# A depthwise convolution divided differently among TensorE, VectorE and ScalarE with GpSimd, in two state-space layers

## The chip, the cores and the metric

The kernel runs on one core of a Trainium2 chip, in fp32 but for a few bf16 operands. The metric is the device time of one execution in microseconds (us). The kernel before took 1493.69 us, the median of three runs (1493.68 to 1497.0). A profile is one further execution; its times are used for the stages.

## The reference, cut to what matters

Two layers are applied in turn to an image of 64 x 64 pixels with 96 channels. Each normalizes its input, projects it to 192 channels `x_val` and 192 gates `z`, convolves `x_val` with its own 3 x 3 filter in each channel, takes `silu`, runs four selective scans over the pixels, normalizes, multiplies by `silu(z)`, projects back and adds the input. The change concerns the projection, the convolution and the gates:

```python
xz = x @ in_proj_w
x_val, z = (xz[..., :D_INNER], xz[..., D_INNER:])
xc = jnp.transpose(x_val, (0, 3, 1, 2))
xc = jax.lax.conv_general_dilated(xc, conv_w, (1, 1), 'SAME', dimension_numbers=('NCHW', 'OIHW', 'NCHW'), feature_group_count=D_INNER) + conv_b[None, :, None, None]
x_val = jax.nn.silu(jnp.transpose(xc, (0, 2, 3, 1)))
...
y = y * jax.nn.silu(z)
return y @ out_proj_w
```

## The kernel before, in words

**Stages.** The program is one serial course: loading, `head` of layer 0, `near_scans` (the scans of layer 0, in a short form), `tail`, `head` of layer 1, `scans` (the long main part) and `last_tail`. Both heads are the same code, called with `l` = 0 and 1. In the profile a head begins with the first `in` matmul, at 23.84 us for layer 0 and at 204.83 us for layer 1.

**Tiles of a head.** The 192 channels times 4096 pixels are three blocks `b` of 128 partitions (64 channels, upper and lower half of the image), each in four chunks `c` of 512 pixels (eight rows). So there are twelve chunks (b, c). For each:

- `project(b, c)` multiplies the input by the weights `ws` on TensorE into a PSUM bank from `room` (tile `in`). `room` has two banks, tags `p0` and `p1`, one buffer each.
- `padded(b, c)` copies that bank into `pad[b]`, which has a border of one pixel on each side. ScalarE does it but for two chunks, which VectorE does.
- `borders(b)`, once for a block, brings the border rows from the neighbouring half or chunk with four DMAs on SP's queue, issued once the block's last `padded` is done.
- The nine taps of the convolution are done in one of three ways. `tap_pe` (TensorE): nine matmuls of shifted views of `pad` with diagonal weights `diag`, summed in a bank (tile `cp`). `tap_dve` (VectorE): nine multiply-adds into a PSUM accumulator `acc` (two buffers). `tap_act` and `tap_pool`: ScalarE multiplies a shifted view into a tile `tap` (three buffers), GpSimd adds it to the chunk's sum. The taps are ordered with the centre row first; taps 3 to 8 read border rows.
- `silu` (ScalarE) takes the sum to `u[b]`.
- `gate(b, c)` is a second projection on TensorE into a bank (tile `z`); `gated(b, c)` takes its `silu` on ScalarE (tile `sz`, eight buffers) and writes it to `szd` in DRAM over SP's queue.

**Shares before.** TensorE convolves chunks 0, 1, 2 of block 2, VectorE chunks (0, 0) to (0, 3) and (1, 0), (1, 1), in pairs, ScalarE with GpSimd (2, 3), (1, 3) and (1, 2). Projections take the banks by `c % 2`; all `cp` tiles are in `p0`, all gates in `p1`. Gates stand between the taps of TensorE, in the ratio of four to nine.

**What sets the order.** Every step of `head` is entered with `at(t, step, ...)`, t being a planned time in about microseconds. At the end the steps are sorted by t and issued; `Ordered` (line 271, which is why the profile puts these instructions on L271) keeps each engine's queue in that order. [...]

**What follows a head.** It returns six `start_y` products on GpSimd (`y = u * ds`, 128 x 1024 each). In layer 0 `near_scans` issues them after its own GpSimd memsets; in layer 1 `scans` issues them first of all. After that come the first matmuls on `u`: `nu` in layer 0, `pj` in layer 1. At the start of `scans`, `su` is made on VectorE (tile `wl` ahead of it) and spread to `du` by DMAs on GpSimd's queue; `sp` is spread to `dt` on SP's queue; GpSimd makes a part of the operands `bT` of the scans. The scans proper are tile `h` on VectorE.

Of the kernel before, what the change touches and what calls it, by code (L numbers as in the profile page):

```python
# [25 lines left out]
HT = TC // 2  # L26
NCH = L // TC
SR = HT // HW
# [16 lines left out]
def two_ss2d_layers(  # L45
# [60 lines left out]
    for h in range(2):  # L106
        t = const.tile([128, 128], F32, name=f"wide{h}")
# [117 lines left out]
    def layer_weights(l, queue):  # L225

        w = {"st": st[l], "next": st[1]}
        w["ipw"] = wts.tile([DM, 2 * DI], F32, name=f"ipw{l}")
        queue.dma_start(out=w["ipw"], in_=ipw[l])
        v = w["v"] = wts.tile([128, 3, NV], F32, name=f"v{l}")  # L230
        op = w["op"] = wts.tile([128, 3, DM], F32, name=f"op{l}")
        for half in HALF:
            queue.dma_start(out=v[half], in_=vec[l].rearrange("(b p) n -> p b n", b=3))
        for half in HALF:
            queue.dma_start(out=op[half], in_=opw[l].rearrange("(b p) n -> p b n", b=3))
        w["ds"] = wts.tile([128, 3], F32, name=f"ds{l}")
        nc.vector.reduce_sum(w["ds"], v[:, :, V_D : V_D + 4], axis=AX.X)
        return w
# [26 lines left out]
    class Ordered:  # L265
# [7 lines left out]
    pe, act, dve, pool, sp = (  # L273
        Ordered(e) for e in (nc.tensor, nc.scalar, nc.vector, nc.gpsimd, nc.sync)
    )
# [991 lines left out]
    def head(l, xT, w):  # L1267

        ipw_s, v, ds = w["ipw"], w["v"], w["ds"]
        with ExitStack() as sc:  # L1270
# [4 lines left out]
            pad = [cv.tile([128, NCH, SR + 2, HW + 2], F32, name=f"pad{l}_{b}") for b in range(3)]  # L1275
# [13 lines left out]
            W2 = HW + 2  # L1289

            def room(name, tag):
                return cvp.tile([128, HT], F32, tag=f"p{tag}", name=name)
# [21 lines left out]
            live = {}  # L1314

            def project(b, c):
                ps = live["in", b, c] = room(f"in{l}_{b}_{c}", c % 2)
                for h, half in enumerate(HALF):
                    g = 2 * c + h
                    pe.matmul(  # L1320
                        ps[half], ws[:, 64 * b : 64 * b + 64], xT[:, g * 512 : (g + 1) * 512],
                        start=True, stop=True,
                    )

            def padded(b, c):
                copy = dve.tensor_copy if (b, c) in ((0, 2), (0, 1)) else act.copy
                copy(
                    pad[b][:, c, 1 : SR + 1, 1 : HW + 1],
                    live.pop(("in", b, c)).rearrange("p (r w) -> p r w", w=HW),
                )  # L1330
# [9 lines left out]
                sp.dma_start(out=t[h1, :n, SR + 1, row], in_=t[h0, 1:, 1, row])  # L1340

            def gate(b, c):
                ps = live["z", b, c] = room(f"z{l}_{b}_{c}", 1)
                for h, half in enumerate(HALF):
                    g = 2 * c + h
                    pe.matmul(
                        ps[half], ws[:, DI + 64 * b : DI + 64 * b + 64],
                        xT[:, g * 512 : (g + 1) * 512], start=True, stop=True,
                    )
# [8 lines left out]
            def weight(b, i, j):  # L1358
                k = V_CW + 3 * i + j
                return v[:, b, k : k + 1]  # L1360

            def source(b, s, i, j):
                return pad[b][:, s, i : i + SR, j : j + HW]
# [9 lines left out]

            def tap_pe(b, c, k):
                if k == 0:
                    live["cp", c] = room(f"cp{l}_{b}_{c}", 0)
                i, j = taps[k]
                pe.matmul(
                    live["cp", c].rearrange("p (r w) -> p r w", w=HW), diag[:, 3 * i + j, :],
                    source(b, c, i, j), start=(k == 0), stop=(k == 8),  # L1380
                )

            def tap_dve(b, c, k):
                i, j = taps[k]
                o = i * W2 + j
                if k == 0:
                    live["acc", b, c] = cvp.tile(
                        [128, 3 * HT], F32, tag="acc", name=f"acc{l}_{b}_{c}", bufs=2
                    )[:, 0 : 2 * SR * W2]
                acc = live["acc", b, c]  # L1390
                acc = acc.rearrange("p (c t) -> p c t", c=2)[:, :, 0 : SR * W2 - 2]
                of = pad[b].rearrange("p c r w -> p c (r w)")[:, c : c + 2, o : o + SR * W2 - 2]
                wk = weight(b, i, j)
                if k == 0:
                    dve.tensor_scalar_mul(acc, of, wk)
                else:
                    dve.scalar_tensor_tensor(acc, of, wk, acc, ALU.mult, ALU.add)
# [15 lines left out]
            def at(t, step, *args):  # L1413
                steps.append((t, len(steps), partial(step, *args)))

            t = 0.0
            for b, order in ((0, (2, 3, 1, 0)), (2, (3, 2, 1, 0)), (1, (3, 2, 1, 0))):
                for c in order:
                    at(t, project, b, c)
                    at(t + 1.0, padded, b, c)  # L1420
                    t += 1.0
                at(t + 0.05, borders, b)

            for n in range(39):
                c, k = divmod(n * 9 // 13, 9)
                if n * 9 % 13 < 9:
                    at(t, tap_pe, 2, c, k)
                    if k == 8:
                        at(t + 1.0, silu, 2, slice(HT * c, HT * (c + 1)), partial(whole, ("cp", c)))
                else:  # L1430
                    z = n - (n * 9 // 13 + 1)
                    at(t, gate, z // NCH, z % NCH)
                    at(t + 0.95, gated, z // NCH, z % NCH)
                t += 0.87

            t = 2.6
            for b, c, k0, k1 in (
                (0, 2, 0, 3), (0, 0, 0, 3), (0, 2, 3, 9), (0, 0, 3, 9), (1, 0, 0, 9)
            ):
                for k in range(k0, k1):  # L1440
                    at(t, tap_dve, b, c, k)
                    t += 1.35
                if k1 == 9:
                    at(
                        t + 0.1, silu, b, slice(HT * c, HT * (c + 2)),
                        lambda b=b, c=c: live.pop(("acc", b, c)).rearrange(
                            "p (c r w) -> p c r w", r=SR, w=W2
                        )[:, :, :, 0:HW],
                    )

            t = 6.6
            for b, c, k0, k1 in (
                (2, 3, 0, 3), (1, 3, 0, 3), (2, 3, 3, 9), (1, 3, 3, 9), (1, 2, 0, 9)
            ):
                for k in range(k0, k1):
                    if k == 0 and (b, c) == (1, 3):
                        t = 10.6
                    at(t - 1.5, tap_act, b, c, k)
                    if k:
                        at(t, tap_pool, b, c, k)  # L1460
                        t += 1.33
                if k1 == 9:
                    at(t + 0.1, silu, b, slice(HT * c, HT * (c + 1)), partial(whole, ("sum", b, c, 0)))

            for _, _, step in sorted(steps, key=lambda at: at[:2]):
                step()
            return [
                partial(start_y, pool.tensor_scalar_mul, ds, b, slice(HT * c, HT * (c + 2)))
                for b, c in ((2, 2), (0, 2), (1, 2), (2, 0), (0, 0), (1, 0))
            ]  # L1470

    def tail(l, w, xT):
# [242 lines left out]
    for l in range(2):  # L1715

        w = ahead.pop("w") if l else layer_weights(0, nc.sync)
        sw = list(zip(*[scan_weights(l, 0, nc.sync)] + ([ahead.pop("sw")] if l else [])))

        later = head(l, ones, w)  # L1720
        xp.close()
        if l:
            sums = ctx.enter_context(
                tc.tile_pool(name="pps", bufs=1, space=PSUM, reuse_waits="tile")
            )
            ready = {}
            scans(sw, sums, ready, later)
        else:
            covered = near_scans(sw, later)
            with tc.If(covered < 1):  # L1730
                for T in range(3):
                    start_y(nc.scalar.mul, w["ds"], T)
                far_scans(sw)
        xp = ExitStack()
        xT = xp.enter_context(tc.tile_pool(name=f"xT{l + 1}", bufs=1, reuse_waits="tile")).tile(
            [DM + 1, L], F32, name=f"xT{l + 1}"
        )
        if not l:
            nc.gpsimd.memset(xT[DM : DM + 1], 1.0)
        ones, xT = xT, xT[0:DM]  # L1740
        last_tail(w, xT, sums, ready) if l else tail(l, w, xT)
# [80 lines left out]
```

## Time and profile before

| what | value |
|---|---|
| median of three runs | 1493.69 us |
| profiled execution | 1506.71 us |
| its span | 1504.9 us |
| TensorE (PE) busy | 1240.2 us, 82% |
| VectorE (DVE) busy | 1323.0 us, 88% |
| ScalarE (ACT) busy | 1215.3 us, 81% |
| GpSimd (POOL) busy | 1213.3 us, 81% |
| head of layer 0, first `in` to last `cp` | 23.84 to 86.3 us |
| head of layer 1, first `in` to last `cp` | 204.83 to 267.3 us |
| two-chunk tap on VectorE (`acc`), x54 in both heads | 1.32 us each |
| one-chunk tap on ScalarE (`tap`), x54 | 0.71 us each |
| its addition on GpSimd, x48 | 1.27 us each |
| `silu` of a gate (`sz`), x24 | 0.60 us each |

The profile names an instruction by line, engine, operation, output tile <- input tiles, shapes and count. A tile's buffer number is left out: `cp` stands for every bank of a convolution on TensorE. A fp32 matmul appears as two instructions. "<-ACT u" after an idle time names what ended the wait. The chain of work that ended last follows back, from the last instruction, what released each step. The busy shares are over the whole span, most of which are the scans; what a change in a head is worth has to be read in the head.

### The profile page before, as it was taken

The page shows a single profiled execution, that of the slowest core. Times are in us where ns is not written, and L with a number is a line of the kernel's source. Part 1 is how long each engine was busy: PE and PEld are TensorE (multiplying, and loading weights), DVE is VectorE, ACT ScalarE, POOL GpSimd, SP SyncE. Part 2 cuts the span into 40 slices and gives each one's busy share as a digit, 9 for nine tenths or more (in the row PEclk, how much of TensorE's full clock was granted, in tenths as well). Part 3 has the DMA queues.
Part 4 walks back from the last instruction along what each step waited for, and adds up shares of the span by engine and source line. Part 5 has one row for each costly group of instructions (what it writes and reads, how often), then busy time and mean ns, then how long its engine had stood idle before and what let it go on. Part 6 is the DMA issues. An engine that isn't in the chain of part 4 may idle for free.

```text
span 1504.9 us, 17294 instructions
## 1 busy us (share of the span) xinstructions
PE 1240.2 (82%) x5047; PEld 475.1 (32%) x5047; DVE 1323.0 (88%) x909; ACT 1215.3 (81%) x2504; POOL 1213.3 (81%) x667
## 2 busy tenths in 40 slices
PE   5974869598888888887888888887988887887887
PEld 2243312233332323232323233333333332332332
DVE  5738675569989998999999999999999999999996
ACT  4755336669979897999999989999898998897873
POOL 2753026759889988998989899898989898989895
PEclk8985979779889988999999999999999999999999
DMA  3222622513435343544435262626262626262634
GB/s 105 69 74 50 145 51 74 138 35 86 112 79 119 94 104 82 116 98 100 114 85 127 72 144 68 151 60 143 56 143 58 140 59 140 58 152 63 149 91 120
DMA packets 85556, 147.70 MB, mean 98 GB/s; under 512 B 33436, under 2 KB 36700, under 8 KB 85356
## 3 DMA queue, kind: packets, MB, share of 16 engines
q1 hardware_dynamic: 83772, 143.96, 39.6%
q0 software_dynamic: 576, 1.57, 0.5%
q10 hardware_dynamic: 1104, 0.98, 0.2%
q8 instruction: 41, 0.67, 0.2%
q14 instruction: 63, 0.52, 0.1%
HBM read 80.85 MB, written 12.13 MB: 62 GB/s over the span
## 4 chain that ended last, share of the span: by engine, by line
DVE 26%; issue 21%; PE 12%; POOL 11%; ACT 10%; DMA 6%; SPq 3%; DVEq 0%; POOLq 0%; ACTq 0%
DVE h L751 16%; DVE b L751 8%; POOL hc L751 7%; ACT a L751 3%; DMA cb<-C 3%; PE pj L751 3%; ACT bT L751 2%; PE ys L751 2%; SPq L751 2%; PE cp L271 2%; PE b L751 2%; POOL sp L751 2%; DMA szt<-szd 2%; POOL ln L751 1%; DMA dt<-sp 1%
## 5 line engine op out<-in xcount | busy, mean ns | idle before, releaser
L751 POOL TENSOR_TENSOR hc<-h,cb 128x1024 f32<-128x1024 f32 x384 | 903.1, 2371 | 104.2 <-DVE h L751 42.1
L751 DVE TENSOR_TENSOR_SCAN h<-a,carry,b 128x1024 f32<-128x1024 f32 x288 | 665.3, 2338 | 31.1 <-PE b L751 8.2
L751 ACT ACTIVATE a<-dt,am 128x1024 f32<-128x1024 f32 x384 | 437.8, 1140 | 59.3 <-DVE h L751 56.8
L751 PE MATMUL ys<-hc,fold 128*64 128x512 f32 x1536 | 430.5, 640 | 0.9 <-POOL hc L751 0.6
L751 ACT ACTIVATE bT<-duT,BT 128x192 f32<-128x192 f32 x1012 | 386.8, 445 | 3.6 <-PE b L751 1.5
L751 PE MATMUL b<-ident,bT 128*128 128x128 f32 x1536 | 224.9, 289 | 36.3 <-DVE h L751 19.9
L751 DVE TENSOR_TENSOR b<-b,du 128x1024 f32<-128x1024 f32 x192 | 232.0, 1208 | 14.0 <-PE b L751 12.0
L751 PEld LDWEIGHTS b<-ident,bT 128*128 128x128 f32 x1536 | 177.9, 147 | 163.0 <-DVE h L751 89.9
L751 DVE TENSOR_TENSOR_SCAN h<-a,b 128x1024 f32<-128x1024 f32 x96 | 216.4, 2278 | 13.7 <-POOL hc L751 3.9
L751 PE MATMUL b<-B,selh 96*128 96x512 bf16 x384 | 117.6, 388 | 125.4 <-DVE h L751 124.7
L751 PEld LDWEIGHTS ys<-hc,fold 128*64 128x64 f32 x1536 | 78.0, 138 | 141.9 <-issue 104.2
L271 POOL TENSOR_TENSOR tap<-tap,tap 128x512 f32<-128x512 f32 x48 | 61.0, 1272 | 63.1 <-ACT tap L271 61.4
L751 PEld LDWEIGHTS <-selh 96*128 96x128 bf16 x384 | 25.7, 98 | 253.3 <-DVE h L751 199.1
L751 PE MATMUL pj<-u,xw 64*124 64x512 f32 x192 | 98.9, 663 | 3.6 <-ACT B L751 1.2
L271 DVE SCALAR_TENSOR_TENSOR acc<-pad,v,acc 128x1052 f32<-128x1052 f32 x48 | 62.9, 1318 | 1.5
L271 PE MATMUL cp<-pad,diag 128*128 128x512 f32 x108 | 58.8, 664 | 5.3 <-ACT u L271 3.1
L751 ACT CAST B<-pj 96x512 bf16<-96x512 f32 (+2 forms) x96 | 54.9, 575 | 7.8 <-PE pj L751 7.8
L751 PE MATMUL ys<-y,ident 128*128 128x512 f32 (+1 forms) x120 | 59.9, 600 | 0.0
L751 POOL TENSOR_TENSOR sp<-sp,ln 128x512 f32<-128x512 f32 x45 | 57.9, 1286 | 0.2
L751 POOL TENSOR_TENSOR ln<-ln,w 128x512 f32<-128x512 f32 x45 | 57.8, 1284 | 0.0
L751 POOL TENSOR_TENSOR su<-sp,u 128x512 f32<-128x512 f32 x45 | 57.6, 1280 | 0.0
L751 PEld LDWEIGHTS pj<-u,xw 64*124 64x124 f32 x192 | 35.0, 197 | 63.5 <-issue 48.6
(188 smaller groups left out, 1208.8 us busy)
## 6 DMA issues: line engine op xcount, KB each, us to landing
cb<-C SPq DMA_DIRECT2D x256, 256.0 KB
dt<-sp SPq DMA_DIRECT2D x192, 128.0 KB
du<-su SPq DMA_DIRECT2D x180, 128.0 KB
szd<-sz SPq DMA_DIRECT2D x24, 256.0 KB
szt<-szd SPq DMA_DIRECT2D x24, 256.0 KB
xT<-xs SPq DMA_DIRECT2D x8, 384.0 KB
xs<-xT SPq DMA_DIRECT2D x1, 1536.0 KB
xs<-xT SPq DMA_DIRECT2D x8, 192.0 KB
```

What stands on the lines that cost most here:

```text
L271: return lambda *args, **more: tc.keep_in_program_order(op(*args, **more))
L751: return lambda *args, **more: tc.keep_in_program_order(op(*args, **more))
```

## The change

The same code is used for both heads. TensorE convolves two chunks instead of three, (2, 3) and (2, 2), in turns of three and six taps and each in a bank of its own. VectorE convolves seven instead of six: block 1 and the lower two chunks of block 0 in pairs, then (2, 0) alone, so that its last nine instructions are half as wide. ScalarE with GpSimd make (0, 3), (0, 2) and (2, 1). Blocks are projected in the order 1, 0, 2 instead of 0, 2, 1, in banks by `(c + c // 2) % 2`; VectorE does one `padded` copy instead of two. The twelve gates stand behind the convolution on TensorE and take both banks in turn. `start_y` goes through the pairs in another order. The planned times t are set anew.

```diff
             def project(b, c):
-                ps = live["in", b, c] = room(f"in{l}_{b}_{c}", c % 2)
+                ps = live["in", b, c] = room(f"in{l}_{b}_{c}", (c + c // 2) % 2)
...
             def padded(b, c):
-                copy = dve.tensor_copy if (b, c) in ((0, 2), (0, 1)) else act.copy
+                copy = dve.tensor_copy if (b, c) == (1, 2) else act.copy
...
             def gate(b, c):
-                ps = live["z", b, c] = room(f"z{l}_{b}_{c}", 1)
+                ps = live["z", b, c] = room(f"z{l}_{b}_{c}", c % 2)
...
             def tap_pe(b, c, k):
                 if k == 0:
-                    live["cp", c] = room(f"cp{l}_{b}_{c}", 0)
+                    live["cp", c] = room(f"cp{l}_{b}_{c}", c % 2)
...
             def tap_dve(b, c, k):
                 i, j = taps[k]
-                o = i * W2 + j
+                o, n = i * W2 + j, 1 if b == 2 else 2
...
-                    )[:, 0 : 2 * SR * W2]
+                    )[:, 0 : n * SR * W2]
                 acc = live["acc", b, c]
-                acc = acc.rearrange("p (c t) -> p c t", c=2)[:, :, 0 : SR * W2 - 2]
-                of = pad[b].rearrange("p c r w -> p c (r w)")[:, c : c + 2, o : o + SR * W2 - 2]
+                acc = acc.rearrange("p (c t) -> p c t", c=n)[:, :, 0 : SR * W2 - 2]
+                of = pad[b].rearrange("p c r w -> p c (r w)")[:, c : c + n, o : o + SR * W2 - 2]
...
-            t = 0.0
-            for b, order in ((0, (2, 3, 1, 0)), (2, (3, 2, 1, 0)), (1, (3, 2, 1, 0))):
-                for c in order:
+            t = 2.5
+            for b in (1, 0, 2):
+                for c in (2, 3, 1, 0) if b == 1 else (3, 2, 0, 1):
                     at(t, project, b, c)
-                    at(t + 1.0, padded, b, c)
-                    t += 1.0
-                at(t + 0.05, borders, b)
-
-            for n in range(39):
-                c, k = divmod(n * 9 // 13, 9)
-                if n * 9 % 13 < 9:
+                    at(t + 1.6, padded, b, c)
+                    t += 1.15
+                at(t + 0.5, borders, b)
+
+            for c, k0, k1 in ((3, 0, 3), (2, 0, 3), (3, 3, 9), (2, 3, 9)):
+                for k in range(k0, k1):
                     at(t, tap_pe, 2, c, k)
-                    if k == 8:
-                        at(t + 1.0, silu, 2, slice(HT * c, HT * (c + 1)), partial(whole, ("cp", c)))
-                else:
-                    z = n - (n * 9 // 13 + 1)
-                    at(t, gate, z // NCH, z % NCH)
-                    at(t + 0.95, gated, z // NCH, z % NCH)
-                t += 0.87
-
-            t = 2.6
+                    t += 0.95
+                if k1 == 9:
+                    at(t + 0.3, silu, 2, slice(HT * c, HT * (c + 1)), partial(whole, ("cp", c)))
+            for b in range(3):
+                for c in range(NCH):
+                    at(t, gate, b, c)
+                    at(t + 1.3, gated, b, c)
+                    t += 1.06
+
+            t = 6.3
             for b, c, k0, k1 in (
-                (0, 2, 0, 3), (0, 0, 0, 3), (0, 2, 3, 9), (0, 0, 3, 9), (1, 0, 0, 9)
+                (1, 2, 0, 3), (1, 0, 0, 3), (1, 2, 3, 9), (1, 0, 3, 9), (0, 0, 0, 9), (2, 0, 0, 9)
             ):
+                n = 1 if b == 2 else 2
                 for k in range(k0, k1):
                     at(t, tap_dve, b, c, k)
-                    t += 1.35
+                    t += 0.77 if b == 2 else 1.33
...
-            t = 6.6
+            t = 10.6
             for b, c, k0, k1 in (
-                (2, 3, 0, 3), (1, 3, 0, 3), (2, 3, 3, 9), (1, 3, 3, 9), (1, 2, 0, 9)
+                (0, 3, 0, 3), (0, 2, 0, 3), (0, 3, 3, 9), (0, 2, 3, 9), (2, 1, 0, 9)
             ):
                 for k in range(k0, k1):
-                    if k == 0 and (b, c) == (1, 3):
-                        t = 10.6
                     at(t - 1.5, tap_act, b, c, k)
                     if k:
-                        at(t, tap_pool, b, c, k)
-                        t += 1.33
+                        at(t + 0.01, tap_pool, b, c, k)
+                        t += 1.29
...
-                for b, c in ((2, 2), (0, 2), (1, 2), (2, 0), (0, 0), (1, 0))
+                for b, c in ((1, 2), (1, 0), (2, 2), (0, 2), (0, 0), (2, 0))
```

More of the change, by code (lines that the diff above doesn't have):

```diff
@@ L1414, in at @@
                 steps.append((t, len(steps), partial(step, *args)))
-            t = 0.0
-            for b, order in ((0, (2, 3, 1, 0)), (2, (3, 2, 1, 0)), (1, (3, 2, 1, 0))):
-                for c in order:
+            t = 2.5
+            for b in (1, 0, 2):
+                for c in (2, 3, 1, 0) if b == 1 else (3, 2, 0, 1):
                     at(t, project, b, c)
-                    at(t + 1.0, padded, b, c)
-                    t += 1.0
-                at(t + 0.05, borders, b)
-            for n in range(39):
-                c, k = divmod(n * 9 // 13, 9)
-                if n * 9 % 13 < 9:
-                    at(t, tap_pe, 2, c, k)
-                    if k == 8:
-                        at(t + 1.0, silu, 2, slice(HT * c, HT * (c + 1)), partial(whole, ("cp", c)))
-                else:
-                    z = n - (n * 9 // 13 + 1)
-                    at(t, gate, z // NCH, z % NCH)
-                    at(t + 0.95, gated, z // NCH, z % NCH)
-                t += 0.87
-            t = 2.6
+                    at(t + 1.6, padded, b, c)
[3 more added lines that the diff above has]
+                for k in range(k0, k1):
+                    at(t, tap_pe, 2, c, k)
+                    t += 0.95
[7 more added lines that the diff above has]
+            t = 6.3
             for b, c, k0, k1 in (
-                (0, 2, 0, 3), (0, 0, 0, 3), (0, 2, 3, 9), (0, 0, 3, 9), (1, 0, 0, 9)
+                (1, 2, 0, 3), (1, 0, 0, 3), (1, 2, 3, 9), (1, 0, 3, 9), (0, 0, 0, 9), (2, 0, 0, 9)
             ):
+                n = 1 if b == 2 else 2
                 for k in range(k0, k1):
                     at(t, tap_dve, b, c, k)
-                    t += 1.35
+                    t += 0.77 if b == 2 else 1.33
                 if k1 == 9:
                     at(
-                        t + 0.1, silu, b, slice(HT * c, HT * (c + 2)),
+                        t + 0.1, silu, b, slice(HT * c, HT * (c + n)),
                         lambda b=b, c=c: live.pop(("acc", b, c)).rearrange(
```

## The prediction

> **What bounds the kernel now.** I read the profile from the end backwards. First the chain of work that ended last, in order of time, around the end of the second head:
>
> ```profile
> 264.35 1.01 PE z L271 x4
> 265.36 1.93 PE cp L271 x4
> 267.29 0.02 issue
> 267.31 0.70 ACT u L271
> 268.01 0.04 issue
> 268.05 1.12 PE pj L751 x2
> ```
>
> The chain stays on TensorE through taps (`cp`, 1.92 us for two) and gates (`z`, 1.01 us each); the scans' first matmul `pj` follows the last `silu` at once. Next the busy time by stretch, for the second head: its projections, its middle and its end.
>
> ```profile
> 204.80:224.00 19.20, 15.78 (x48) 3.65 (x48) 14.54 (x13) 9.89 (x18) 5.12 (x5) 0.75 0.12 25
> 224.00:247.40 23.40, 22.61 (x52) 6.53 (x52) 22.05 (x17) 16.41 (x25) 16.09 (x13) 0.85 0.19 66
> 247.40:268.10 20.70, 19.14 (x52) 5.58 (x51) 0.91 (x1) 11.00 (x18) 9.29 (x9) 1.00 0.23 89
> ```
>
> The columns after the length are PE, PEld, DVE, ACT, POOL, then TensorE's granted clock, and DMA. In the last 20.7 us VectorE is nearly empty (0.91 us) and TensorE full: TensorE has work that VectorE could do. The first head shows the same in the timelines of TensorE and VectorE (start, length, then in brackets the wait before):
>
> ```profile
> 43.06 1.51 PE L271 MATMUL cp<-pad,diag 128*128 128x512 f32 x2 [1.12 <-ACT pad L271]
> ...
> 59.90 1.13 PE L271 MATMUL cp<-pad,diag 128*128 128x512 f32 x2 [0.78 <-ACT u L271]
> ...
> 86.15 4.09 PE L271 MATMUL nu<-u,wide 128*128 128x192 f32 x24
> 88.83 0.56 DVE L271 COPY nus<-nu 128x384 f32<-128x384 f32 x1 [22.42 <-ACT nus L271]
> ```
>
> TensorE convolves and gates from 43.06 to 86.3; the near scans' `nu` follows without a gap. Last, GpSimd at the start of the scans:
>
> ```profile
> 268.10 17.72 POOL L271 TENSOR_SCALAR y<-u,ds 128x1024 f32<-128x1024 f32 x6 [8.85 <-ACT u L271]
> 285.76 4.30 POOL L751 DMA_DIRECT2D du<-su  x8
> ```
>
> The six `start_y` products wait 8.85 us for the last `silu`, then hold the `du` transfers behind them until 285.76, though the first `su` was there at 280.26.
>
> [...] 0.50 at 44 to 46 us, after the thin end of the projections, and full from about 50, so about 6.5 us of dense work here. [...] The taps read one SBUF operand and a PSUM accumulator, and beside GpSimd's adds they vary only from 1308 to 1320 ns[...] A `wl` subtraction with two SBUF inputs took 1490 instead of 693 ns beside `start_y`[...]
>
> **The change, part by part** (times of the first head; the second has the same offsets, 181.0 us later).
>
> *VectorE.* It gains nine one-chunk taps and loses one `padded` copy (0.69). Two-chunk taps take 1.319 us for 1052 elements; 512-element scalar-tensor-tensor operations take 0.75, so I take 0.77 for 526: 9 x 0.77 = 6.9 us. Taps start at 28.18, as now. 27 x 1.333 = 36.0, two waits of about 0.5 (border rows of block 1; accumulator, below): 65.1, then 72.0. VectorE is not last.
>
> *TensorE, removed.* Nine taps: 9 x 0.96 = 8.6 us. Two waits for the single `cp` bank (each 0.78) go, since the two chunks have a bank each.
>
> *Projections.* Twelve, in banks taken in turn, before and after with one pair on the same bank. Each waits for the `padded` copy two places earlier, and ScalarE does eleven of these instead of ten, with `tap_act` between. Step by step: (1,0) is copied at 31.8, (0,3) at 33.6, (0,2) at 35.4, (0,1) at 38.9. The fourth tap of (0,3) now stands on ScalarE ahead of three copies of block 2, and needs the border rows of block 0, whose transfers are issued only when (0,1) is copied. Before, the corresponding tap ran 3.9 us after the first issue with no wait: so at most 3.9; at least 2.4 (two issues of 0.6, then 1.1 until DMA activity). I take 3.0: the tap at 42.0, copies of (2,2) at 42.6 and (2,0) at 43.7, the last projection at 43.3 (half clock, 1.8) and its copy done at 45.8. The first `cp` then starts at 45.8 instead of 43.06: a loss of 2.7, between 2.1 and 3.6. The border rows of block 2 are covered by the six centre taps.
>
> *TensorE's taps.* 18, of which some 6.5 us at half clock as before: 3.4 taps at 1.9, 14.6 at 0.96, so 45.8 + 6.5 + 14.0 = 66.3. ScalarE meanwhile sits before the `silu` of (2,3) until 60.5, and GpSimd starves some 3 us. That costs GpSimd, not the end; but `silu` of (2,2) comes at 67.0, and the first gate needs its bank: 67.7.
>
> *Gates.* Twelve in a row, behind the taps, 1.01 each when not held. A bank returns when ScalarE has read it (0.60); four taps and two `silu` stand between. I count 12.5 us: 80.2. Before, TensorE ended at 86.3: 6.0 us saved in each head. The taps between gates, which hid ScalarE's reads, are gone; if ScalarE holds each gate 0.3 longer, 3.6 us are lost again.
>
> *Last `silu` (2,0).* VectorE has it at 72.0, ScalarE issues it behind the last gate, 81.4. `nu` of blocks 0 and 1 don't need it; hidden by 4 us of `nu` matmuls.
>
> *SP's queue.* The twelve `szd` writes move behind all border transfers, about 1.1 us apart instead of 3.2. SP needs 0.32 each. The next transfers on SP, the near scans' C rows, come some 12 us after the last: hidden. Their data, 12 x 256 KB, at the 220 GB/s seen at 281 to 300 us take 14 us, also done before.
>
> *GpSimd.* Its adds end at about 75. In the first head the memset of `nxd` still waits for the last gate, so nothing more comes of this. In the second head `start_y` can start there: five products of 2.85 us end at 89.5, the sixth at 92.3, against 104.8. `su` of block 0 comes at 99.3 - 6.2 = 93.1, so `du` is issued when `su` is there. Now it is 5.5 us behind. At the least this gives nothing (dt, du and cb keep the DMAs at 207 to 240 GB/s from 281 to 302, so landing may be bound by data); at the most 4.7: the last operand of the second scan, GpSimd's `bT` at 296.01, could start with `duT` at 290.7, and the next block's `pj`, which waits for it, with it. I take 4.0.
>
> **Sum.** First head 6.0, second head 6.2, start of the scans 4.0: 16.2 us. Everything between and after is a serial course of the same instructions, so the shift stays. The profiled execution took 1506.71 us, of which 1504.9 are the span; it becomes 1490.5. The median of the runs is 13.0 lower; the stages here carry the same work there, so I take the difference over: 1493.7 - 16.2 = 1477.5, say 1478.
>
> **Rivals.**
>
> *A: as summed, 1478.* Own range 1471 to 1485, from the border rows (0.6 each way in a head), the gates' hold (up to 1.8 a head) and 0 to 4.7 at the scans.
>
> *B: a head balanced as its schedule lists it, 1468.* If TensorE gets its clock at once (3.1 less) and ScalarE is then early at the `silu` of (2,2) (0.7), and the border rows are fast (0.6), a head ends 4.4 earlier: 8.8 in all, 1469; VectorE's 72.0 plus its `silu` is the floor. For it: the projections keep TensorE's matmuls close; against: at 44 to 50 the clock was halved after less sparse work.
>
> *C: little gained, 1488.* Border rows at their late end, half clock some 2 us longer, gates held 0.15 each, and the start of the scans bound by DMA: (6.0 - 0.6 - 1.0 - 1.8) x 2, with nothing from GpSimd: 5.2 us.
>
> *D: slower, 1505.* One mechanism: the clock. The change thins TensorE's work ahead of the taps (a projection every 2 us with 1.08 of work) and again at the gates. If the gate stays at half through the taps, 14.6 taps cost 0.94 more each, 13.7 us, and a head ends 7.7 later than now; less 4 at the scans, 11.4 slower: 1505. It decides from 6.0 / 0.94, six more taps at half clock. For it: 0.50 from 44 to 50. Against: the clock came back within 6.5 us of dense work, and 18 taps without a wait are dense.
>
> *The change may not do what it says* only in part: built, the queues of TensorE, VectorE, ScalarE and GpSimd hold the new order, so this gets no chance of its own.
>
> **Chances.** A 0.58, B 0.22, C 0.10, D 0.10. 0.3% is 4.5 us, about what a measurement of this kernel can tell from no change; faster thus means under 1489.2. A, B and over half of C lie there: 0.86; the rest of C is the same, 0.04; D slower, 0.10. The range reaches from inside B to C's middle, 1466 to 1488; it leaves out D, half of C and the far end of B, together about 0.2.
>
> **What would show it.** First `cp` near 45.8, last gate's end near 80, VectorE's last tap near 72, `start_y` of the second head before its end, no VectorE tap over 1.35 us, `du` issued as soon as `su` exists. It is wrong if the first `cp` comes after 48, if the clock is at half for over 10 us from there, if the gates take over 15 us, or if the head's gain is given back between `pj` and the fifth scan.

## The result and the profile after

| | before | after |
|---|---|---|
| median of four runs | 1493.8 us (1493.68 to 1497.0) | 1471.72 us (1468.69 to 1476.09) |
| ratio, 95% interval | | 0.985 (0.982 to 0.988) |
| profiled execution, its span | 1506.71, 1504.9 | 1471.02, 1469.2 |

The change saves 22 us, 1.5%. The forecast was 1478. Where the time went is read from the stages: each is the distance between the first instructions named at the head of a column, in us. The last two rows are the changed kernel in two further executions, made beside experiments: the second with a median of 1472.56 us in six runs, ratio 0.982 (0.978 to 0.986), the third with the one given under (11). The kernel before has one execution on record with its stages.

| execution | head 0: `in` to `nu` | `nu` to last `nv` | last `nv` to `m` | tail: `m` to `in` | head 1: `in` to `pj` | `pj` to third `pj` | rest |
|---|---|---|---|---|---|---|---|
| before | 62.3 | 19.8 | 50.7 | 48.2 | 63.2 | 41.5 | 1195.3 |
| after | 50.4 | 22.3 | 53.2 | 48.7 | 50.0 | 37.0 | 1184.0 |
| after, second | 51.5 | 22.3 | 50.6 | 48.1 | 50.9 | 36.8 | 1188.8 |
| after, third | 50.3 | 22.3 | 53.0 | 48.8 | 50.1 | 37.0 | 1196.6 |

The heads are 11.9 and 13.2 us shorter, the start of the scans 4.5; the stretch between the heads is 5.5 longer, 2.5 of it before the last `nv`; these 2.5 stand in all three executions of the changed kernel, the others in two of them. Together that is -24.1, against -22.1 of the medians. The rest of the scans differs by 12.6 us between executions of one and the same kernel (1184.0, 1188.8, 1196.6), so its 11.3 between before and after can't be put down to the change. For the same reason the experiments below are read by their stages first.

The chain of work that ended last, at the end of the second head:

```profile
241.89 1.10 PE z L271 x4
...
244.20 0.59 ACT sz L271
...
245.96 0.32 ACT sz L271
...
246.32 1.94 PE z L271 x8
248.26 3.75 PE pj L751 x12
```

The taps are gone from the end. Only gates are left on TensorE, and in these lines the chain passes twice over to ScalarE's `sz`, which has to give a bank back. The same head by stretch: projections, taps, gates (PE, PEld, DVE, ACT, POOL, clock, DMA share, GB/s).

```profile
198.17:217.09 18.92, 14.24 (x48) 3.20 (x48) 14.97 (x12) 10.99 (x20) 7.24 (x6) 0.86 0.12 24
217.09:235.72 18.63, 17.15 (x36) 7.32 (x36) 18.21 (x15) 15.24 (x22) 16.56 (x14) 0.92 0.06 14
235.72:248.19 12.47, 11.89 (x49) 2.64 (x49) 9.56 (x12) 9.92 (x17) 11.33 (x8) 1.00 0.53 202
```

VectorE, 0.91 us busy in the last stretch before, is now busy for 9.56 of 12.47. The first head in the timelines of TensorE and VectorE, and then GpSimd at the end of the second:

```profile
42.82 17.24 PE L271 MATMUL cp<-pad,diag 128*128 128x512 f32 x36 [0.69 <-ACT pad L271]
61.55 10.18 PE L271 MATMUL z<-xT,ws 97*64 97x512 f32 x40 [1.49 <-ACT u L271]
...
74.01 4.20 PE L271 MATMUL nu<-u,wide 128*128 128x192 f32 x24
...
64.67 6.41 DVE L271 SCALAR_TENSOR_TENSOR acc<-pad,v,acc 128x526 f32<-128x526 f32 x8
```

```profile
243.52 17.27 POOL L271 TENSOR_SCALAR y<-u,ds 128x1024 f32<-128x1024 f32 x6
260.74 2.27 POOL L751 DMA_DIRECT2D du<-su  x4
```

Eighteen taps in a row take 17.24 us, with a wait of 1.49 before the gates; VectorE's last tap ends at 71.08, 3 us before the last gate. `start_y` now begins without a wait 4.7 us before `pj` (248.19), where it began with it, and `du` goes out at 260.74, 1.1 us after the first `su` is done (259.60); before, it was 5.5.

### The profile page after: what moved, and what is told of

It is laid out like the page before. It is cut to its first block, busy times and chain, and to the rows that moved or that the text cites. A ratio compares the mean times of both kernels' runs of the same rounds, so it can differ in the third digit from the quotient of the medians.

```text
span 1469.2 us, 17235 instructions
## 1 busy us (share of the span) xinstructions
PE 1205.7 (82%) x5011; PEld 469.7 (32%) x5011; DVE 1338.4 (91%) x925; ACT 1216.5 (83%) x2506; POOL 1211.8 (82%) x667
## 4 chain that ended last, share of the span: by engine, by line
DVE 28%; issue 22%; PE 11%; POOL 11%; ACT 9%; DMA 6%; SPq 2%; DVEq 0%; POOLq 0%; ACTq 0%
DVE h L751 18%; DVE b L751 8%; POOL hc L751 7%; DMA cb<-C 4%; ACT a L751 3%; PE ys L751 3%; ACT bT L751 2%; SPq L751 2%; PE pj L751 2%; POOL sp L751 2%; PE b L751 1%; POOL ln L751 1%; DMA xT<-xs 1%; PE cp L271 1%; DMA dt<-sp 1%
## 5 line engine op out<-in xcount | busy, mean ns | idle before, releaser
L751 PE MATMUL pj<-u,xw 64*124 64x512 f32 x192 | 94.1, 635 | 2.2 <-DVE w L751 1.2
L271 DVE SCALAR_TENSOR_TENSOR acc<-pad,v,acc 128x1052 f32<-128x1052 f32 (+1 forms) x64 | 75.2, 1181 | 2.1
L751 ACT CAST B<-pj 96x512 bf16<-96x512 f32 (+2 forms) x96 | 54.9, 575 | 4.5 <-PE pj L751 4.5
L751 POOL TENSOR_TENSOR ln<-ln,w 128x512 f32<-128x512 f32 x45 | 57.6, 1280 | 0.0
L751 PE MATMUL pd<-xd,dwb 29*64 29x512 f32 x192 | 54.7, 639 | 0.0
```

What stands on the lines that cost most here:

```text
L271: return lambda *args, **more: tc.keep_in_program_order(op(*args, **more))
L751: return lambda *args, **more: tc.keep_in_program_order(op(*args, **more))
```

## The experiments

All are edits of the changed kernel. Ratios are to the kernel before, on the same chip, with their 95% intervals. My theory after reading the two traces: a head gains by the work taken from TensorE and by the two banks, the gain is limited by the wait for the border row and by ScalarE's queue, and a part is given back in the near scans by two tiny operations on VectorE. The rivals are in the expectations.

### One part alone: the shares (1)

Convolution in bank 0 and gates in bank 1, taps and gates in turn as before; the chunks of after.

```diff
-                    live["cp", c] = room(f"cp{l}_{b}_{c}", c % 2)
+                    live["cp", c] = room(f"cp{l}_{b}_{c}", 0)
...
-                ps = live["z", b, c] = room(f"z{l}_{b}_{c}", c % 2)
+                ps = live["z", b, c] = room(f"z{l}_{b}_{c}", 1)
...
-            for c, k0, k1 in ((3, 0, 3), (2, 0, 3), (3, 3, 9), (2, 3, 9)):
-                for k in range(k0, k1):
+            for n in range(30):
+                i, o = divmod(n, 5)
+                if o % 2 == 0:
+                    i = 3 * i + o // 2
+                    c, k = 3 - i // 9, i % 9
...
+                else:
+                    z = 2 * i + o // 2
+                    at(t, gate, z // NCH, z % NCH)
...
```

> The changed kernel's shares, project order and VectorE and GpSimd lists, but TensorE arranged as before: both cp tiles in one bank, all gates in the other and standing between the taps, three taps to two gates. Theory, the gain is the chunk moved off TensorE: nine taps at 0.96 us and one bank wait of 0.8 us, so a head is about 53 us long (62.3 before, 50.2 after) and the time 1476 to 1479 us. Rival, the gain is the order and the banks: a head stays over 58 us and the time is 1487 to 1492 us.

Measured: 1482.7 us, ratio 0.992 (0.989 to 0.995). The heads take 53.4 and 54.9 us: 8.9 and 8.3 shorter than before, of 11.9 and 13.2. In TensorE's timeline the single bank shows in the middle of the head:

```profile
59.25 1.13 PE L271 MATMUL cp<-pad,diag 128*128 128x512 f32 x2 [2.08 <-ACT u L271]
```

The second chunk can't begin before ScalarE has read the first. So the chunk taken from TensorE, with the new projection order and the new lists of VectorE, ScalarE and GpSimd that this run keeps, is worth two thirds to three quarters of a head's gain, and the order and banks on TensorE the last 3 to 5 us of a head. The time is 4 us above the range expected by the theory: the second head was 54.9 us instead of 53, and the start of the scans took 40.0 us instead of 37.0, which the theory had left out.

### The other part alone: order and banks (2)

TensorE keeps three chunks, the third, (2, 0), behind the other two in bank 1; VectorE makes six. Gates behind the convolution.

```diff
-                    live["cp", c] = room(f"cp{l}_{b}_{c}", c % 2)
+                    live["cp", c] = room(f"cp{l}_{b}_{c}", c % 2 if c else 1)
...
-            for c, k0, k1 in ((3, 0, 3), (2, 0, 3), (3, 3, 9), (2, 3, 9)):
+            for c, k0, k1 in ((3, 0, 3), (2, 0, 3), (3, 3, 9), (2, 3, 9), (0, 0, 9)):
...
-                (1, 2, 0, 3), (1, 0, 0, 3), (1, 2, 3, 9), (1, 0, 3, 9), (0, 0, 0, 9), (2, 0, 0, 9)
+                (1, 2, 0, 3), (1, 0, 0, 3), (1, 2, 3, 9), (1, 0, 3, 9), (0, 0, 0, 9)
```

> The changed kernel's orders and banks, gates behind the convolution, but chunk (2,0) is convolved by TensorE (three chunks) and not by VectorE (six). Theory, the moved chunk is the gain: nine taps at 0.87 us more on TensorE's path in each head, 7.8 us, so a head is about 58 us long and the time 1486 to 1490 us. Rival, order and banks are the gain: a head of 52 to 54 us, time 1475 to 1479 us.

Measured: 1486.63 us, ratio 0.995 (0.992 to 0.998). Heads 57.6 and 56.5 us: 4.7 and 6.7 shorter than before, 7.2 and 6.5 longer than after. The 27 taps run in one piece:

```profile
43.42 25.14 PE L271 MATMUL cp<-pad,diag 128*128 128x512 f32 x54 [0.69 <-ACT pad L271]
```

The third chunk costs 25.14 - 17.24 = 7.9 us, 0.88 a tap. The two parts together, 13.6 and 15.0 us, are 1.7 and 1.8 more than the whole. Both runs keep the projection order and banks, the `padded` copies and the chunks of ScalarE with GpSimd of the changed kernel, so what these are worth is counted in both; no run takes them apart.

### The gates' second bank taken away (3), and TensorE kept busy (4)

```diff
-                ps = live["z", b, c] = room(f"z{l}_{b}_{c}", c % 2)
+                ps = live["z", b, c] = room(f"z{l}_{b}_{c}", 1)
```

> The changed kernel with all gates in bank 1, the convolution still in two banks. Theory (the second bank is what lets the next gate run while a product is read): a gate's pitch rises from 1.04 us to the sum of its matmuls and the product, 0.85 and some 0.7 with the hand-over, about 1.6 to 1.8; twelve gates take 19 to 21 us instead of 12.5; each head 7 to 9 us longer, time about 1487. Rival (the order behind the convolution does it, banks matter little): twelve gates in 13 to 14 us, time 1473.

Measured: 1503.82 us, ratio 1.006 (1.004 to 1.009), 31 us slower than after beside it (1472.56) and slower than before. Twelve gates take 29.6 and 28.3 us. TensorE's timeline in the first head, and its two stretches of gates:

```profile
62.34 1.08 PE L271 MATMUL z<-xT,ws 97*64 97x512 f32 x4 [0.95 <-ACT sz L271]
64.12 1.72 PE L271 MATMUL z<-xT,ws 97*64 97x512 f32 x4 [0.70 <-ACT sz L271]
66.53 1.97 PE L271 MATMUL z<-xT,ws 97*64 97x512 f32 x4 [0.69 <-ACT sz L271]
69.20 1.98 PE L271 MATMUL z<-xT,ws 97*64 97x512 f32 x4 [0.70 <-ACT sz L271]
```

```profile
60.31:66.50 6.19, 3.88 (x13) 0.59 (x12) 6.01 (x7) 4.42 (x9) 5.59 (x5) 0.83 0.23 86
66.50:89.90 23.40, 17.70 (x36) 2.66 (x36) 4.06 (x6) 7.58 (x12) 2.53 (x2) 0.50 0.27 101
```

The pitch is 1.78 us (62.34 to 64.12), as the theory had it, until a gate's matmuls go from 1.08 to 1.98 us; then it is 2.67. The clock fell to 0.50, and it stayed there to the end of the head, though TensorE is busy 17.70 of 23.40 us. The expectation had missed this. To separate the bank from the clock, half a gate more was put behind each gate, into bank 0, where nobody reads it; the edit of (3) stays:

```diff
+                pe.matmul(
+                    room(f"idle{l}_{b}_{c}", 0)[HALF[0]], ws[:, DI + 64 * b : DI + 64 * b + 64],
+                    xT[:, 0:512], start=True, stop=True,
+                )
```

> All gates in bank 1 as in the run with one bank, and after each gate one more pair of matmuls of half a gate into bank 0, which nobody reads; the output is unchanged, TensorE has more to do. Theory (with one bank the wait for the product leaves TensorE idle enough for its clock to be halved, and that halved clock is 0.9 of the 2.67 us of a gate's pitch): full clock through the gates, pitch about 1.8 us, twelve gates in about 21.5 us instead of 29.6 and 28.3, time about 1488. Rival (the pitch is 2.67 us for the bank's sake, and the clock is a by-product or is halved anyway): 29 us or more for twelve gates, time 1504 or above.

Measured: 1490.87 us, ratio 0.995 (0.993 to 0.998): with half as much again to do, TensorE is through the twelfth gate after 21.2 us instead of 29.6.

```profile
66.22 1.08 PE L271 MATMUL z<-xT,ws 97*64 97x512 f32 x4
67.13 1.02 PE L271 MATMUL idle<-xT,ws 97*64 97x512 f32 x2
68.00 1.08 PE L271 MATMUL z<-xT,ws 97*64 97x512 f32 x4
```

The pitch is 1.78 us, 1.83 at the last two gates, and the clock 1.00 to the end. So of the 17 us that one bank costs twelve gates (29.6 against 12.5), about 8.7 are the wait for the bank (21.2 - 12.5) and 8.4 the clock that this wait brings down from 1.00 to 0.50 (29.6 - 21.2). Rival D of the prediction is this mechanism; here it set in with a wait of 0.7 us in each gate, which the second bank takes away.

### The two scalings in the near scans, on ScalarE (5)

`decays` multiplies two tiles of 128 x 24 (`am`) by constants, on VectorE. For layer 0 they were moved to ScalarE.

```diff
-    def decays(am):
+    def decays(am, scale=nc.vector.tensor_scalar_mul):
...
-            nc.vector.tensor_scalar_mul(a[:, 1, 0:D], a[:, 0, 0:D], -0.5)
-            nc.vector.tensor_scalar_mul(a[:, 0, 0:D], a[:, 0, 0:D], -1.0)
+            scale(a[:, 1, 0:D], a[:, 0, 0:D], -0.5)
+            scale(a[:, 0, 0:D], a[:, 0, 0:D], -1.0)
...
-            am = decays(weights[2])[0]
+            am = decays(weights[2], act.mul)[0]
```

> The changed kernel with one edit: the two products that scale am in the near scans (2.91 and 2.79 us on VectorE in the changed kernel, 0.17 and 0.18 us before) are done by ScalarE. Theory, [...]they waited for a start_y product each, which now runs beside them; the near stage from nu to the tail's first m, 75.5 us against 70.5 us before, becomes 2.5 to 5 us shorter and the time 1467 to 1469 us. Rival, the longer near stage comes from TensorE's granted clock there (0.63 against 0.66) and the two products are beside the path: 1471 to 1472 us.

Measured: 1467.6 us, ratio 0.982 (0.978 to 0.986). VectorE's timeline, first before, then after, then run (1):

```profile
96.89 0.17 DVE L247 TENSOR_SCALAR am<-am 128x24 f32<-128x24 f32 x1
97.09 0.18 DVE L248 TENSOR_SCALAR am<-am 128x24 f32<-128x24 f32 x1
```

```profile
84.85 2.91 DVE L247 TENSOR_SCALAR am<-am 128x24 f32<-128x24 f32 x1
87.80 2.79 DVE L248 TENSOR_SCALAR am<-am 128x24 f32<-128x24 f32 x1
```

```profile
86.70 2.05 DVE L247 TENSOR_SCALAR am<-am 128x24 f32<-128x24 f32 x1
```

With the edit the last `nv` starts 19.7 us after `nu`, against 19.8 before and 22.3 in after. Without the edit it is 22.3 in eight of nine executions, of after and of the other runs, and 21.3 in (1), where the first scaling took 2.05 us; in the four executions with the edit it is 19.7: the saving of 2.5 us is shown. The median of the runs, 4 us under after's, says no more than that.

The reason isn't shown. GpSimd does six products `y<-u,ds` beside this, of 2.83 us each, from 76.42 on: the fourth begins at about 84.9, the fifth at 87.7, the sixth at 90.5 (its start in the list of tile `y`). The first scaling begins at a boundary between two of them and ends with the fourth, the second ends with the fifth: each takes as long as a whole product. It isn't the boundary that counts: in (1) and (3) the first scaling began 0.8 and 0.7 us into a product and still ended with it, after 2.05 and 2.14 us. But before, the same scalings ran 1.3 and 1.5 us into a product (87.14 + 3 x 2.84 = 95.7 to 98.5) in 0.17 and 0.18 us. What decides it isn't settled.

### `start_y` held back (6)

`start_y` takes pair (2, 0), the last to be ready, first.

```diff
-                for b, c in ((1, 2), (1, 0), (2, 2), (0, 2), (0, 0), (2, 0))
+                for b, c in ((2, 0), (1, 2), (1, 0), (2, 2), (0, 2), (0, 0))
```

> The changed kernel with one edit: of the six start_y products the one of pair (2,0), whose silu is the last, comes first, so that GpSimd starts them only at the head's end, as before. Theory, the early start_y lets du go early and saves 4.5 us at the start of the scans (first pj to third pj 37.0 us after, 41.5 before): the time is 1475 to 1477 us and that stage 41 us again. Rival, the stage is bound by its DMAs or by the granted clock: 1471 to 1472.5 us and the stage 37 us.

Measured: 1472.92 us, ratio 0.985 (0.981 to 0.990). In GpSimd's timeline the products wait for ScalarE again:

```profile
247.78 16.94 POOL L271 TENSOR_SCALAR y<-u,ds 128x1024 f32<-128x1024 f32 x6 [6.09 <-ACT u L271]
264.67 4.80 POOL L751 DMA_DIRECT2D du<-su  x9
```

From `pj` (246.34) that is `du` at +18.3 us instead of +12.6, and the third `pj` at +39.8 instead of +37.0. In these two profiles the early `start_y` is worth 2.8 of the 4.5 us that the start of the scans gained. Of the other 1.7, 0.8 stand in one `wl` subtraction on the chain, which the first `dt` transfer waits for as well: it took 1.49 us beside a `start_y` product before, 0.69 in this run and in after. The last 0.9 stay without a cause. The time lies under the 1475 to 1477 of the theory: in this profile the stretch from the last `nv` to `m` took 50.4 us, in that of after 53.2, which makes up for the 2.8; what it took in the other runs isn't known.

### The border wait hidden (7), and with the scalings (8)

In after, ScalarE's fourth product of (0, 3) waits for the border rows of block 0, with copies of block 2 behind it:

```profile
39.80 0.72 ACT L271 ACTIVATE tap<-pad,v 128x512 f32<-128x512 f32 x1 [1.74 <-DMA pad<-pad]
```

The next copy on ScalarE starts at 40.43 us, though its projection had ended by 39.19.

The product is queued behind those copies in run (7); run (8) adds the edit of (5).

```diff
-                    at(t - 1.5, tap_act, b, c, k)
-                    if k:
-                        at(t + 0.01, tap_pool, b, c, k)
+                    ready = 16.8 if b == 0 and k > 2 else 0.0
+                    at(max(t - 1.5, ready), tap_act, b, c, k)
+                    if k:
+                        at(max(t, ready) + 0.01, tap_pool, b, c, k)
```

> The changed kernel, but ScalarE's products of chunk (0,3) from its fourth tap on are queued behind all copies of block (2, ...), so that the wait for block 0's border row (1.74 us in the changed kernel's first head) has three copies ahead of it. Theory (the border wait stands in the serial course of the head): first convolution matmul 1.5 to 2 us earlier after the first projection in each head (19.2 to about 17.5 us), the head 1 to 2 us shorter (50.4 to about 49), the time about 1469, since the half clock then meets more of the taps. Rival (GpSimd's additions or the block's own border row take over): the first matmul moves, but the last gate doesn't, head within 0.5 us of 50.4, time 1471.

> The changed kernel with two edits: the border wait hidden behind the copies of block (2, ...) in both heads, and the two scalings of the decay constants in the first near stage on ScalarE instead of VectorE. If both readings hold: heads 49 us each, the part of the near stage up to the last nv 19.8 us instead of 22.3, time about 1465 to 1467. If the first near stage's saving is given back by the granted clock further on: near stage still 75 us, time about 1469.

Measured: 1473.79 us, ratio 0.986 (0.982 to 0.990), and 1473.95 us, ratio 0.985 (0.981 to 0.989), beside after with 1472.56: no gain. Heads of 50.2 and 51.9, and of 50.8 and 51.8 us. TensorE's timeline in run (7), and its clock from the start of the gates on:

```profile
39.78 15.72 PE L271 MATMUL cp<-pad,diag 128*128 128x512 f32 x36 [0.69 <-ACT pad L271]
59.07 12.23 PE L271 MATMUL z<-xT,ws 97*64 97x512 f32 x40 [3.57 <-ACT u L271]
```

```profile
59.07:63.40 4.33, 4.33 (x12) 1.20 (x12) 4.22 (x4) 1.81 (x4) 3.50 (x3) 0.50 0.16 61
```

The first tap starts 16.4 us after the first projection instead of 19.2, with nothing but the order in ScalarE's queue changed; that is more than I had put down, and the taps need 15.72 us, at full clock (1.00) throughout. Then all of it is lost: TensorE stands for 3.57 us until ScalarE reaches the `silu` of (2, 2), queued behind three products and another `silu`, which waited 0.37 us for GpSimd, and returns at half clock (0.50 in the line above). The rival held.

Run (8) kept the 19.7 us up to the last `nv`, but both runs took 40.4 us from `pj` to the third `pj` instead of 37.0. There ScalarE stands 5.0 us before its first `a` in run (8):

```profile
264.57 1.15 ACT L751 ACTIVATE a<-dt,am 128x1024 f32<-128x1024 f32 x1 [5.04 <-issue]
```

The view names no releaser, but the landings in the traces do: in all fourteen executions the first `a` begins 0.15 us after the fourth `dt` transfer has landed. That transfer landed 6.0 and 6.1 us after its issue in (7) and (8), where the first `du` had been issued 0.6 us before it; 3.4 us in after, where both were issued at the same moment; 2.3 us before and in (6), where `du` came over 4 us later. The same three groups hold in all fourteen executions: 5.9 to 6.1, 3.3 to 3.5, 2.3. In (7) and (8) the first `dt` was issued 0.8 us later than in after, since the `wl` subtraction met a `start_y` product again and took 1.49 us. So where the first `du` went out 0.6 us ahead, the `dt` that the scans need first landed 2.6 us later than where both went out together.

### The `silu` moved ahead (9), repeated (10) beside after (11)

Run (8), with TensorE's taps listed 0.8 us apart instead of 0.95, the `silu` of (2, 3) 2.1 us behind its last tap, the gates where they were, and the `silu` of (2, 2) listed with its last tap, so that it stands ahead of the products of (2, 1).

```diff
-                    t += 0.95
+                    t += 0.8
                 if k1 == 9:
-                    at(t + 0.3, silu, 2, slice(HT * c, HT * (c + 1)), partial(whole, ("cp", c)))
+                    at(t + (2.1 if c == 3 else -0.3), silu, 2, slice(HT * c, HT * (c + 1)), partial(whole, ("cp", c)))
+            t += 2.7
             for b in range(3):
```

> The kernel with both edits (border wait hidden, scalings on ScalarE), and the silu of chunk (2,2) moved ahead of the taps of chunk (2,1) on ScalarE's queue, where it comes up as the convolution ends. Theory (with the border wait hidden, TensorE stands 3.6 us before the gates for a silu that is queued behind taps which GpSimd paces, and comes back at half clock): first gate 2 to 3 us earlier, the wait before it under 1.5 us, the gates in 12.5 us instead of 14.5, the last gate 2 to 4 us earlier; then VectorE's last tap (70.8) and its silu are late next, and the near stage begins at about 72 instead of 73.6 to 74.6: heads 48.5 to 49.5 us instead of 50.8 and 51.8, time about 1469. Rival (ScalarE's queue as a whole paces the gates): the first gate comes earlier, the last one doesn't, heads within 0.5 us of 50.8 and 51.8, time 1474.

> The kernel with three edits (border wait hidden, scalings on ScalarE, silu of chunk (2,2) ahead of taps) once more, beside the changed kernel on one chip. If its stages hold: heads 49 to 49.5 us and the near stage up to the last nv 19.8 us, together some 5 us under the changed kernel: time about 1466. If the gain of the earlier run was a draw of the granted clock: heads or near stage within 1 us of the changed kernel's, time 1471.

> The changed kernel itself, to measure the three edits against: time 1471 to 1473, heads 50 to 51.5 us, near stage up to the last nv 22.3 us with the two scalings at 2.9 and 2.8 us.

Measured: 1466.13 us, ratio 0.978 (0.975 to 0.981); again 1468.2 us, 0.980 (0.976 to 0.984), beside after with 1476.35 us, 0.985 (0.981 to 0.989). TensorE's timeline in run (9):

```profile
56.94 1.94 PE L271 MATMUL z<-xT,ws 97*64 97x512 f32 x8 [0.78 <-ACT u L271]
59.87 2.21 PE L271 MATMUL z<-xT,ws 97*64 97x512 f32 x8 [0.99 <-ACT sz L271]
```

Heads 49.4 and 48.9 us, then 48.5 and 48.9, with 50.3 and 50.1 for after beside it; 19.7 us up to the last `nv` in both against 22.3; 36.3 and 36.2 from `pj` to the third `pj` against 37.0. That is 6.3 us by the stages for the repeated pair. The medians differ by 8, and the intervals of their ratios overlap a little. The theory's half is right: the wait before the gates is 0.78 and the clock stays at 1.00 through them. The rival's half too: twelve gates now take 15.6 us instead of 12.5, since ScalarE, between two `sz`, still has products to make for GpSimd. At the gates ScalarE's queue is the bound of a head now.

## Why the prediction was right, and where its terms were off

The forecast, 1478 in 1466 to 1488, lies 6 us above 1471.72. Its mechanism was right and two sizes were off, in opposite directions. It summed 16.2 us; the stages gained 29.6 (11.9 + 13.2 + 4.5) and gave 5.5 back. That the total came so close is in part luck: the two heads gained 12.9 us more than the 12.2 put down for them, and a loss of 5.5 that the forecast had put at nothing took part of that away.

*"The first `cp` then starts at 45.8 instead of 43.06."* It started at 42.82. Three terms: the copy of (0, 1) was done at 38.06, not 38.9; the border wait "I take 3.0" was 1.74; and from that product to the first tap 3.0 us passed, not 3.8, since the last projection ran at 1.08 us, at full clock (1.00), where 1.8 had been put down. Together 3.0 us a head. My lower bound of the border wait, 2.4, was too high as well: it had been put together from two issues and the delay of a DMA's activity on other rows.

*"Some 6.5 us at half clock as before: 3.4 taps at 1.9, 14.6 at 0.96."* The taps took 17.24 us instead of 20.5. Half clock (0.50) covered their first 3.1 us in this profile, to 45.9; before, it had lasted 6.8 us, from 43.7 to 50.5. Against the 6.5 put down that gives back half of 3.4; and a tap that follows a tap takes 0.87 us (eighteen in 15.72 in run (7), all at full clock), where 0.96 came from pairs between gates: 18 x 0.09 = 1.6. The second is a flaw of the working: the row measured another neighbourhood. The first is a draw, as the changed kernel's second execution shows beside after (first two lines after, then the second execution, same code in this stage):

```profile
42.65:45.85 3.20, 3.03 (x4) 1.48 (x5) 3.16 (x3) 2.68 (x5) 2.82 (x3) 0.50 0.24 52
45.85:49.05 3.20, 3.20 (x8) 1.35 (x8) 3.13 (x3) 2.83 (x3) 3.04 (x4) 0.99 0.11 23
```

```profile
42.65:45.85 3.20, 2.82 (x4) 1.27 (x5) 3.13 (x4) 2.89 (x5) 2.81 (x3) 0.50 0.23 49
45.85:49.05 3.20, 3.20 (x5) 1.25 (x4) 3.13 (x3) 2.63 (x3) 3.04 (x4) 0.50 0.12 25
```

TensorE is dense from 42.82 and from 43.03 us on. In after the clock was at 0.50 from 42.5 to 45.9 us, for 3.4 us, in the second execution from 42.3 to 49.1, for 6.8. The other runs show the same two lengths: in the sixteen heads with eighteen or 27 taps in a row that meet a stretch of half clock, it lasted 3.4 us where the first tap began at most 0.6 us after the clock had fallen or before that, and 6.8 us in the three where it began 0.7 to 1.5 us after. What sets the length isn't shown. The longer stretch costs 1.5 us (taps of 18.74 us against 17.24).

*The gates: "I count 12.5 us."* 12.5. *The wait before them, 1.4:* 1.49. *VectorE's last tap at 72.0:* 71.08. *`silu` of (2, 0) and SP's queue hidden:* the chain doesn't pass through either. These steps held. So the heads came out as rival B has them, "a head balanced as its schedule lists it": it put a head 4.4 us under A's, and the profile has them 5.9 and 7.0 under. Its terms were sized otherwise: half clock did come, and the way to the first tap gave 3.0 us where B had 0.6.

*"Start of the scans 4.0"* in the sum. 4.5 in the stages, of which (6) gives 2.8 to the early `start_y` and 0.8 to a `wl` subtraction that the prediction had seen at 1490 ns but not counted: the number is better than its reason.

*"Everything between and after is a serial course of the same instructions, so the shift stays."* This step failed. A shift stays only if all engines shift alike; here GpSimd's memsets, which come after the last gate, start 0.2 us after `nu` (74.20) instead of 1.6 before it (84.52), since TensorE has no taps left behind the gates; so the `start_y` products begin 2.4 us after `nu` instead of 1.0, and VectorE's scalings meet them at another moment. That is 2.5 us, shown by (5); why they are held at the one moment and not at the other is open. The other 2.5, from the last `nv` to `m`, are no part of it: of all fourteen executions, before and the edits among them, eight took 50.3 to 51.2 us there and six 52.6 to 53.2, the changed kernel itself both. The difference goes with TensorE's clock near the end. These lines of the third and the second execution show the same six instructions, which took 2.93 us at a clock of 0.50 in after and 1.56 at 1.00 before:

```profile
141.60 2.93 PE L271 MATMUL ny<-nnhc,fold 128*128 128x256 f32 x6 [2.09 <-DVE nnhc L271]
```

```profile
142.55 1.56 PE L271 MATMUL ny<-nnhc,fold 128*128 128x256 f32 x6 [1.21 <-DVE nnhc L271]
```

The last twelve `ny` instructions took 0.54 us each in all six long executions and 0.34 to 0.41 in the eight short ones.

*Rivals.* C (its late border row and held gates) didn't occur. D was put at a clock that stays down through the taps. It didn't, but (3) shows the mechanism at the gates, one bank away. What brought the clock down there was not the thinness of the projections, but a wait of 0.7 us after 1.08 us of work, repeated: with the wait it was 0.50, with the wait filled, in (4), 1.00.

## What to carry to other kernels

Moving work off the busiest engine is worth what the next wait leaves of it: write down, for each engine, what its queue holds behind the moved step, and look there for the next bound (here ScalarE). A second PSUM bank for a chain of small matmuls was worth nearly twice the wait it removed here (17 us against 8.7), since with that wait TensorE's clock was at 0.50 for the rest of the chain. And a stage whose code is unchanged still has to be checked for who meets whom: a shift of 1.4 us between two engines cost 2.5 us in operations of 0.17, and a transfer issued 0.6 us earlier had another land 2.6 us later.

## What was unexpected of the hardware

- Two VectorE operations on 24 elements per partition took 2.91 and 2.79 us beside GpSimd's products of 2.83 us and ended with them; begun 0.7 to 0.8 us into a product, the first took 2.05 to 2.14 us and ended with it too; begun 1.3 and 1.5 us into one, they took 0.17 and 0.18 us.
- TensorE's clock fell to 0.50 and stayed there for over 23 us of gates in which TensorE was busy for 76% of the time (17.70 of 23.40 us), and stayed at 1.00 with the same waits filled by matmuls that nobody reads.
- After one idle stretch of 3.57 us the clock was at 0.50 in the next 4.3 us; with the waits of 0.78 and 0.99 us in (9) it stayed at 1.00.
- The same transfer (the fourth `dt`, 128 KB) landed 2.3, 3.4 or 6.0 us after its issue, according to whether the first `du` was issued over 4 us after it, with it, or 0.6 us before it.
